# Turning x3 in blocks by way of DRAM, logits one step later, and four scalings on VectorE

## The chip, the cores and the metric

The kernel runs on one core of one Trainium2 chip. The metric is device time in microseconds (us) of the whole program, as the median of several executions. One more execution is taken by the hardware profiler; its views are what the text below quotes. The engines are TensorE (PE, and PEld for its weight loads), VectorE (DVE), ScalarE (ACT), GpSimd (POOL) and SyncE (SP). Each runs its own instructions in order. SP issues most of the DMAs, also in order, so that a DMA that has to wait holds up the ones behind it.

## The reference

A block of four layers on x of 8 x 512 tokens with 1024 features, all in float32. Each layer adds its output to x and begins with a layer norm.

```python
x = x + softmax_attention(layernorm(x), ...)           # 32 heads of 32
x = x + ffn(layernorm(x), weight, bias, centroids, assignments)
x = x + sigmoid_attention(layernorm(x), bv_q, bv_k, bv_v)   # 4 heads of 256, causal
x = x + ffn(layernorm(x), weight, bias, centroids, assignments)

def ffn(x, weight, bias, centroids, assignments):
    dots = softmax(x @ centroids.T / 0.1)              # 64 clusters
    hits = dots > 0.01
    dense = x @ weight.T + bias
    return where(any(hits, axis=1)[:, None] & any(hits, axis=0)[assignments][None, :], dense, 0)
```

In the sigmoid attention, Q, K and V are the normed x times one vector each; scores go through a sigmoid and a causal mask and are multiplied with V, head by head. The ffn needs the logits of every token against 64 centroids, the any() over all tokens of the block, and the dense product.

## The kernel before

The tokens are cut into 32 tiles of 128 (`NTILE`), four to a batch (`TPB`), eight batches. The stages follow each other: the softmax attention (up to about 2600 us), the first dense product with its gate (to about 3000), the sigmoid attention in 33 head steps (about 3001 to 3330), and the second dense product (to the end). x after the first ffn is called x2, after the sigmoid attention x3; both lie in DRAM as rows (`dr.x2`, `dr.x3`) and, after the norm, turned, with features in the partitions (`dr.xT2`, `dr.xT3`).

The change is in the head steps and in their first and last moments. Everything there is issued in the order in which the program is written (manual schedule); waits are put in by the framework, between engines, wherever a tile or a buffer of a pool is shared.

One head step s of the loop over `heads + 1` does this, in this order:

1. `load_head(s + 2)`: four DMAs on SP that bring the turned, normed x2 of a batch for one head (`cxT`, 128 KB each, three buffers).
2. `sig.scores(s)`: sixteen matmuls on TensorE (records "csc", L1300), the sigmoid on ScalarE (`at`, L1305), and four causal selects on POOL (L1308).
3. `by_token`: the second half of the cluster logits of finished tiles (TensorE L333, a copy on ScalarE L336). At the last tile of a batch it hands over the softmax steps (L357 to L380: VectorE, with one exponential on ScalarE, L361, which needs a table load, and the sigmoid after it another one).
4. `sig.keys(s + 1)`: ScalarE scales the turned x by q and k vectors (L1292).
5. `load_x2(s + 4)`: one DMA on SP into a ring of ten.
6. For the x3 tile normed in the step before, `turned`: for an even tile a fetch from DRAM, for an odd one eight transposes on TensorE (L277, "tp") with one copy on VectorE and one on ScalarE, and a store by POOL (L1447).
7. `x3_pieces(s - 5)`: statistics of the next x3 tile on VectorE, its root on POOL (L235), the store of x3 by POOL (L1473), the scaling on VectorE (L243).
8. `sig.values(s - 1)`: twenty records "o" on TensorE (L1319), whose results VectorE adds to x (L1325).
9. `by_cluster`: the first half of the logits (TensorE L325, a copy on ScalarE L329), for two tiles together after an odd tile.
10. `run_held`: softmax steps handed over in 3, and for an even tile the turn in blocks: VectorE turns 32 x 32 blocks of the tile (L294, `box`), and SP writes them to DRAM with four DMAs whose pieces are 128 bytes (L300), so that the tile lies turned in DRAM. The fetch of the next step reads it back.
11. `sig.value(s + 3)`: the scaling of one tile to V (ScalarE L240) and its product with the v vector (POOL L1286).

A tile t is normed in step t + 5 and turned or fetched in step t + 6. `in_blocks(t)` says which tiles go by way of DRAM: the even ones below 25. The logits' accumulators, the transposes and the turned maxima share three PSUM buffers (`ps_m`, tag "mm"). The pools for turned tiles (`Tpool`) and for normed ones (`npool`) have two buffers each.

Before the loop, the last pair of x2 tiles (30 and 31) goes through `x2_pair(15)`: gate, statistics, the factors `kept` (L1461). Its two scalings `n` run in step 1 and its turns in steps 2 and 3. The values of tiles 2 and 3 are made in step 0; those of 0 and 1 earlier, during the last dense product. All of these scalings go through `stage.rescale`, on ScalarE:

```python
def rescale(self, out, x, kept):
    self.nc.scalar.activation(out, x, AF.Identity, scale=kept[0], bias=kept[1])
```

Of the kernel before, what the change touches and what calls it, by code (L numbers as in the profile page):

```python
# [13 lines left out]
F32 = mybir.dt.float32  # L14
# [3 lines left out]
ALU = mybir.AluOpType  # L18
# [4 lines left out]
P = 128  # L23
B, S, H = 8, 512, 1024
NT = B * S
NC = H // P
TPB = S // P
NTILE = NT // P
# [5 lines left out]
HEADS_B, HD_B = 4, 256  # L34
# [34 lines left out]
class Filler:  # L69
# [38 lines left out]
    def run(self, count):  # L108

        while self.queue and count:  # L110
            count -= self._run_one() > 0
# [106 lines left out]
class Stage:  # L218
# [23 lines left out]
    def scale(self, out, x, mv, r, j):  # L242
        self.nc.vector.tensor_scalar(out, x, mv[:, j, 0:1], r[:, j : j + 1], ALU.subtract, ALU.mult)  # L243
# [1016 lines left out]
class SigmoidAttention:  # L1260
# [21 lines left out]
    def value(self, t, x, kept, ring=None):  # L1282
        pool, tag = (self.npools[t // TPB % 2], "n") if ring is None else (ring, "x2")
        v = self.v[t] = pool.tile([P, H], F32, tag=tag, name=f"cn_{t}")
        self.stage.rescale(v, x[t], kept)
        self.nc.gpsimd.tensor_tensor(v, v, self.v_bind, ALU.mult)  # L1286

    def keys(self, b, h):
# [44 lines left out]
def block_body(tc, long, dr, args, out):  # L1333
    x, xT_in, qkvw, qkvb, ow, ob, bv_q, bv_k, bv_v, wT, fbias, cT, assign = args
    nc = tc.nc
# [5 lines left out]
    def pools(stack, side):  # L1341
        def make(name, bufs, space=None):
            extra = dict(space=space) if space is not None else dict(side=side)
            return stack.enter_context(tc.tile_pool(name=name, bufs=bufs, reuse_waits="tile", **extra))

        return make
# [4 lines left out]
    stage, filler = Stage(tc, cst, small, ps_m), Filler()  # L1351
# [39 lines left out]
    kept = fixed.tile([P, 2, NTILE], F32, name="kept")  # L1391
    sel, pairs = {}, NTILE // 2

    def keep(t):
        return kept[:, 0, t : t + 1], kept[:, 1, t : t + 1]

    def dense_pools(stack):
        sb = pools(stack, right)
        return sb("f_load", 2), sb("f_sum", 1), sb("f_u", 4), pools(stack, left)("ps_d", 5, PSUM)
# [3 lines left out]
    dense1 = Dense(stage, weights, dense_pools(dense_stack), None, dr.xT1, dr.x1, hits1, sel)  # L1403
# [22 lines left out]
    a_outer.close()  # L1426

    sb = pools(middle, left)
    xring, npool, Tpool = sb("c_x", 10), sb("c_n3", 2), sb("c_T3", 2)
    dense1.xring = xring  # L1430

    def turned_tile(t, xT_dram):

        st = {}

        def xn():
            if "n" not in st:
                st["n"] = npool.tile([P, H], F32, tag="n3", name=f"n3_{t}")
            return st["n"]

        def xT():
            if "T" not in st:
                st["T"] = Tpool.tile([P, NC, P], F32, tag="T3", name=f"T3_{t}")
            return st["T"]

        def last():
            nc.gpsimd.dma_start(xT_dram[t], st["T"].rearrange("p c t -> p (c t)"))  # L1447

        return xn, xT, last

    def x2_pair(p):

        turns, tiles = [], (2 * p, 2 * p + 1)
        mv, cols = small.tile([P, TPB, 2], F32, tag="ln_mv", name="ln_mv")[:, :2], ts(p, 2)
        for t in tiles:
            dense1.gate(t)
            nc.gpsimd.dma_start(dr.x2[t], dense1.x[t])
        for k, t in enumerate(tiles):
            stage.stats(dense1.x[t], mv[:, k, :])
        stage.rstd(mv, 2, kept[:, 0, cols])  # L1460
        nc.vector.scalar_tensor_tensor(kept[:, 1, cols], mv[:, :, 0], -1.0, kept[:, 0, cols], ALU.mult, ALU.mult)  # L1461
        for t in tiles:
            xn, xT, _ = turned_tile(t, dr.xT2)
            scale = (0.0, lambda xn=xn, t=t: stage.rescale(xn(), dense1.x[t], keep(t)))
            turns.append((scale, stage.block_pieces(xn, xT, dr.xT2[t])))
        return turns

    def x3_pieces(t, blocks=False):


        xn, xT, last = turned_tile(t, dr.xT3)
        norm = stage.norm_pieces(lambda: x2[t], xn)
        norm.insert(1, (0.0, lambda: nc.gpsimd.dma_start(dr.x3[t], x2[t])))  # L1473
        later = held.extend if t < NTILE - TPB else None
        if blocks:
            made = []

            def box():
                if not made:
                    made.append(Tpool.tile([P, NC, P], F32, tag="T3", name=f"B3_{t}"))  # L1480
                return made[0]

            def fetch():
                nc.sync.dma_start(xT().rearrange("p c t -> p (c t)"), dr.xT3[t])

            held.extend(what for _, what in stage.block_pieces(xn, box, dr.xT3[t]))
            return norm, [(0.0, fetch)], hits2.pieces(t, xT, later)
        return norm, stage.turn_pieces(xn, xT, last, vector=(t < NTILE - TPB - 1)), hits2.pieces(t, xT, later)
# [4 lines left out]
    def run_held():  # L1493
        run(enumerate(held))
        held.clear()
# [4 lines left out]
    def load_x2(t):  # L1500
        if t < NTILE:
            x2[t] = xring.tile([P, H], F32, tag="x2", name=f"cx2_{t}")
            nc.sync.dma_start(x2[t], dr.x2[t])

    def load_head(s):
        if s < heads:
            sig.load_head(*divmod(s, HEADS_B), dr.xT2)
# [4 lines left out]
    for p in range(pairs):  # L1512
# [27 lines left out]
        if p > 0:  # L1540
            dense1.sums(p + 1)
        turns = x2_pair(p)
        dense1.load_turned(p + 2)
        dense1.load_x(p + 2)
# [2 lines left out]

    sig.open(pools(sig_stack, left))
    def in_blocks(t):
        return t % 2 == 0 and t < NTILE - TPB - 3  # L1550


    turned, normed, by_token, clustered = None, None, [], []
    for s in range(heads + 1):
        load_head(s + 2)
        if s < heads:
            sig.scores(*divmod(s, HEADS_B))
        run(by_token)
        by_token = []
        if s + 1 < heads:  # L1560
            sig.keys(*divmod(s + 1, HEADS_B))
        if s == 0:
            for t in range(2, TPB):
                sig.value(t, x2, keep(t))
        elif s == 1:
            run([scale for scale, _ in turns])
        load_x2(s + TPB)
        turned, normed = normed, None
        if turned is not None:
            run(turned[0])  # L1570
        if s > HEADS_B:
            t = s - HEADS_B - 1
            norm, *normed = x3_pieces(t, in_blocks(t))
            run(norm)
        if s > 0:
            sig.values(*divmod(s - 1, HEADS_B), x2)
        if turned is not None:
            clustered.append(turned[1])
            if not in_blocks(s - HEADS_B - 2):
                for by_cluster, _ in clustered:  # L1580
                    run([by_cluster])
                by_token = [second for _, second in clustered]
                clustered = []
        run_held()
        if s in (2, 3):
            run(turns[s - 2][1])
        t = s + TPB - 1
        if TPB <= t < NTILE:
            sig.value(t, x2, keep(t))
# [49 lines left out]
@with_exitstack  # L1639
def block_kernel(ctx, tc, x, xT_in, qkvw, qkvb, ow, ob, bv_q, bv_k, bv_v, wT, fbias, cT, assign, out):  # L1640
    long = ctx.enter_context(tc.tile_pool(name="long", bufs=1))
    dram = ctx.enter_context(tc.tile_pool(name="dram", bufs=1, space=DRAM))
    with tc.manual_schedule():
        block_body(tc, long, Scratch(dram), (x, xT_in, qkvw, qkvb, ow, ob, bv_q, bv_k, bv_v, wT, fbias, cT, assign), out)
# [33 lines left out]
```

## Time and profile before

| | |
|---|---|
| median of 3 runs | 3735.04 us (3732.08 to 3738.76) |
| the profiled execution's own time | 3736.19 us |
| its span | 3734.5 us |
| TensorE busy | 3683.2 us, 99% of the span |
| VectorE, ScalarE, POOL busy | 68%, 25%, 16% |
| mean DMA rate | 160 GB/s |

In the profile's lines, "L294 DVE STREAM_TRANSPOSE B<-n" is an instruction of line 294 on VectorE that writes tile B from n. "idle before <-X" tells how long the engine waited and for what. The chain of waits is followed back from the last instruction, at each step to what released it; time on the chain is time that the end depends on. In a table by windows the columns are the busy time of each engine, the granted clock of TensorE, the mean busy share of the 16 DMA engines, and GB/s.

### The profile page before, as it was taken

The numbers are of one execution on the slowest core, as the hardware profiler recorded it, in microseconds if no ns is written. First come the engines' busy times: TensorE is split into PE (matmuls) and PEld (weight loads), VectorE is DVE, ScalarE is ACT, GpSimd is POOL, SyncE is SP. The second block draws the span as 40 slices with busy tenths as digits, with TensorE's granted clock in tenths as the row PEclk, the third lists the DMA queues.
The fourth block names the chain that finished last, engine by engine and source line by source line (L and its number), as shares of the span: only waits on it lengthen the run. The fifth ranks groups of instructions, "written<-read, shape, count | busy, mean of one in ns | idle before, by whom it ended". The sixth has DMA issues, their size and how long they took to land.

```text
span 3734.5 us, 76359 instructions
## 1 busy us (share of the span) xinstructions
PE 3683.2 (99%) x32794; PEld 1877.6 (50%) x32794; DVE 2541.4 (68%) x3495; ACT 925.6 (25%) x1015; POOL 592.4 (16%) x572
## 2 busy tenths in 40 slices
PE   8999999999999999999999999998999999999999
PEld 4444454544545555445445445443444467774444
DVE  4777676777667667766767767665788845556656
ACT  1222222222222222222222222231111144430000
POOL 1222111111111111111111111111000045530000
PEclk9999999999999999999999999999999999999999
DMA  5345445645655455465465454456576667763332
GB/s 172 114 131 170 138 141 148 197 137 153 191 146 153 152 161 169 132 196 155 139 185 156 144 150 121 121 162 228 158 180 179 170 189 234 224 220 131 130 132 99
DMA packets 728641, 598.55 MB, mean 160 GB/s; under 512 B 322152, under 2 KB 574064, under 8 KB 728304
## 3 DMA queue, kind: packets, MB, share of 16 engines
q1 hardware_dynamic: 701072, 496.40, 46.5%
q0 software_dynamic: 22912, 81.54, 5.7%
q10 hardware_dynamic: 4320, 15.73, 1.0%
q8 instruction: 259, 4.24, 0.5%
q14 instruction: 78, 0.64, 0.1%
HBM read 459.30 MB, written 134.25 MB: 159 GB/s over the span
## 4 chain that ended last, share of the span: by engine, by line
PE 92%; DVE 4%; DMA 1%; issue 1%; SPq 1%; ACT 0%; POOL 0%; DVEq 0%; ACTq 0%; POOLq 0%
PE mm L554 41%; PE dense L1238 18%; PE sc L873 7%; PE av L929 6%; PE sc L905 6%; PE o L1319 4%; PE csc L1300 4%; PE sc L902 2%; PE logitsT L325 1%; PE den L941 1%; DVE nmax L874 1%; PE tp L277 1%; DVE sum L918 0%; PE tpm L554 0%; SPq L300 0%
## 5 line engine op out<-in xcount | busy, mean ns | idle before, releaser
L874 DVE TENSOR_REDUCE nmax<-sc 128x4 f32<-128x2048 f32 x256 | 586.0, 2289 | 291.1 <-PE sc L873 291.0
L907 ACT ACTIVATE pT<-sc 128x2048 f32<-128x2048 f32 x256 | 480.9, 1879 | 1131.2 <-PE sc L905 1126.5
L554 PE MATMUL mm<-xT,w 128*64 128x256 f32 (+1 forms) x3736 | 429.6, 384 | 1.1 <-DVE rden L944 1.1
L916 POOL TENSOR_TENSOR sum<-pT,pT 128x1024 f32<-128x1024 f32 x128 | 307.6, 2428 | 754.2 <-ACT pT L907 682.3
L554 PEld LDWEIGHTS mm<-xT,w 128*64 128x64 f32 (+1 forms) x3736 | 242.1, 135 | 206.2 <-issue 56.2
L554 PE MATMUL mm<-s,w 128*32 128x256 f32 (+1 forms) x3672 | 321.2, 381 | 1.4 <-DVE qk L144 1.4
L918 DVE TENSOR_TENSOR sum<-sum,pT 128x2048 f32<-128x2048 f32 x128 | 291.9, 2281 | 0.9 <-ACT pT L907 0.9
L873 PE MATMUL sc<-qk,qk 32*64 32x512 f32 x4096 | 285.1, 613 | 0.5 <-ACT pT L907 0.4
L142 DVE TENSOR_TENSOR u<-dense,u 128x512 f32<-128x512 f32 x223 | 147.9, 684 | 185.1 <-PE dense L1238 169.7
L554 PEld LDWEIGHTS mm<-s,w 128*32 128x32 f32 (+1 forms) x3672 | 180.5, 122 | 180.7 <-issue 69.1
L905 PE MATMUL sc<-qk,qk 32*128 32x512 f32 x2048 | 264.0, 589 | 0.0
L929 PE MATMUL av<-pT,v 128*32 128x512 f32 x2048 | 247.6, 601 | 0.0
L554 PE MATMUL mm<-ow,ctxT 128*32 128x512 f32 (+2 forms) x1276 | 246.5, 599 | 0.3 <-DMA ow<-o_T 0.3
L1238 PE MATMUL dense<-sum,s 128*128 128x512 f32 x512 | 231.8, 593 | 0.0
L554 PEld LDWEIGHTS mm<-w,xT 128*64 128x64 f32 (+1 forms) x3888 | 197.5, 133 | 62.2 <-issue 48.9
L554 PE MATMUL mm<-w,xT 128*64 128x128 f32 (+1 forms) x3888 | 218.1, 274 | 0.0
L144 DVE SCALAR_TENSOR_TENSOR qk<-mm,qkvb_s,qk 128x256 f32<-128x256 f32 x224 | 107.5, 480 | 125.4 <-PE mm L554 120.3
L554 PE MATMUL mm<-ow,c 128*64 128x512 f32 (+2 forms) x864 | 170.4, 596 | 2.7 <-DMA ow<-o_T 2.7
L1238 PE MATMUL dense<-wT_s,dT_b 128*128 128x512 f32 x384 | 171.2, 593 | 0.0
L1238 PE MATMUL dense<-wT_s,dT_a 128*128 128x512 f32 x384 | 171.1, 593 | 0.0
L554 PE MATMUL mm<-w,s 128*64 128x128 f32 x2688 | 162.5, 274 | 0.0
L554 PEld LDWEIGHTS mm<-w,s 128*64 128x64 f32 x2688 | 148.0, 137 | 22.9 <-issue 22.9
(232 smaller groups left out, 4468.2 us busy)
## 6 DMA issues: line engine op xcount, KB each, us to landing
w<-in_qkvw SPq DMA_DIRECT2D x252, 256.0 KB, 3.0
ow<-o_T SPq DMA_DIRECT2D x240, 256.0 KB, 3.6
w<-qk_T SPq DMA_DIRECT2D x224, 256.0 KB, 2.8
ow<-in_ow SPq DMA_DIRECT2D x180, 256.0 KB, 3.1
w<-v_T SPq DMA_DIRECT2D x112, 256.0 KB, 2.7
x<-in_x SPq DMA_DIRECT2D x32, 512.0 KB, 5.1
dT_a<-xT SPq DMA_DIRECT2D x32, 512.0 KB, 6.0
x_a<-x SPq DMA_DIRECT2D x32, 512.0 KB, 6.8
```

Of the source, the lines that this page charges most:

```text
L142: nc.vector.tensor_tensor(out, acc, other, ALU.add)
L554: nc.tensor.matmul(out[cols], lhsT[:, cols], rhs, **flags)
L873: nc.tensor.matmul(sc[ts(j, P // 2), h, :], st["q"][rows, cols], st["k"][rows, :], start=True, stop=True)
L874: nc.vector.tensor_reduce(st["nmax"][:, qt, :], sc, AX.X, ALU.max, negate=True)
L905: nc.tensor.matmul(sc[:, h, :], st["k"][rows, ts(kt, P)], st["q"][rows, :], start=False, stop=True)
L907: nc.scalar.activation(pT, sc, AF.Exp, scale=SCALE_A)
L916: nc.gpsimd.tensor_tensor(st["sum"][:, h, :], st["pT", 0][:, h, :], st["pT", 1][:, h, :], ALU.add)
L918: nc.vector.tensor_tensor(st["sum"], st["sum"], st["pT", kt], ALU.add)
L929: nc.tensor.matmul(st["av"][rows, :], st["v"][:, kt, rows], pT[:, h, :], start=(kt == 0), stop=(kt == TPB - 1))
L1238: nc.tensor.matmul(st["acc"], st["left"][LEFT[k]][:, c, :], self.w[RIGHT[k]][:, c, :], start=(c == 0), stop=(c == half - 1),)
L1300: nc.tensor.matmul(sc[:, AT_OFF[i] : AT_OFF[i] + n], k[:, c, ts(i, P)], xT[:, c, i * P :], start=(c == 0), stop=(c == 1),)
L1319: nc.tensor.matmul(acc[:, j - jj, :], at[:, start : start + P], self.v[b * TPB + i][:, cols], start=(i == 0), stop=(i == j),)
```

## The change

Four edits. All tiles below 25, odd ones too, are turned in blocks by way of DRAM. The box that holds the blocks comes from `npool`, and `Tpool` has three buffers instead of two. The logits of two tiles are still taken together, but after the next even tile has come, so one step later (from tile 25 on as before: at once). And four scalings go from ScalarE to VectorE: the values of tiles 2 and 3, and `n` of tiles 30 and 31.

```diff
     def value(self, t, x, kept, ring=None):
         v = self.v[t] = pool.tile([P, H], F32, tag=tag, name=f"cn_{t}")
-        self.stage.rescale(v, x[t], kept)
+        if 2 <= t < TPB:
+            self.nc.vector.tensor_scalar(v, x[t], *kept, ALU.mult, ALU.add)
+        else:
+            self.stage.rescale(v, x[t], kept)
         self.nc.gpsimd.tensor_tensor(v, v, self.v_bind, ALU.mult)
...
-    xring, npool, Tpool = sb("c_x", 10), sb("c_n3", 2), sb("c_T3", 2)
+    xring, npool, Tpool = sb("c_x", 10), sb("c_n3", 2), sb("c_T3", 3)
...
-            scale = (0.0, lambda xn=xn, t=t: stage.rescale(xn(), dense1.x[t], keep(t)))
+            def scale(xn=xn, t=t):
+                if p < pairs - 1:
+                    stage.rescale(xn(), dense1.x[t], keep(t))
+                else:
+                    nc.vector.tensor_scalar(xn(), dense1.x[t], *keep(t), ALU.mult, ALU.add)
+
+            scale = (0.0, scale)
...
-                    made.append(Tpool.tile([P, NC, P], F32, tag="T3", name=f"B3_{t}"))
+                    made.append(npool.tile([P, H], F32, tag="n3", name=f"B3_{t}").rearrange("p (c t) -> p c t", c=NC))
...
     def in_blocks(t):
-        return t % 2 == 0 and t < NTILE - TPB - 3
+        return t < NTILE - TPB - 3
...
         if turned is not None:
+            t, now = s - HEADS_B - 2, []
+            if t % 2 == 0:
+                now, clustered = clustered, []
             clustered.append(turned[1])
-            if not in_blocks(s - HEADS_B - 2):
-                for by_cluster, _ in clustered:
-                    run([by_cluster])
-                by_token = [second for _, second in clustered]
-                clustered = []
+            if not in_blocks(t):
+                now, clustered = now + clustered, []
+            for by_cluster, _ in now:
+                run([by_cluster])
+            by_token = [second for _, second in now]
```

## The prediction

> **What bounds the kernel now.** I read the page first (busy time, then the chain of waits), then the chain in order of time around the head steps, which the change rewrites, then the timeline at both ends of that stage, then the DMA share there.
>
> ```profile
> PE 3683.2 (99%) x32794; PEld 1877.6 (50%) x32794; DVE 2541.4 (68%) x3495; ACT 925.6 (25%) x1015; POOL 592.4 (16%) x572
> ...
> PE 92%; DVE 4%; DMA 1%; issue 1%; SPq 1%; ACT 0%; POOL 0%; DVEq 0%; ACTq 0%; POOLq 0%
> ```
>
> TensorE is the bound, and a gain must come from TensorE time. The chain in the head steps, one pair of steps:
>
> ```profile
> 3083.37 4.32 PE csc L1300 x16
> 3087.68 0.87 PE tp L277 x8
> 3088.56 4.32 PE o L1319 x20
> 3092.88 1.90 PE logitsT L325 x32
> 3094.77 4.51 PE csc L1300 x16
> 3099.29 0.39 PE logits L333 x4
> 3099.68 4.37 PE o L1319 x20
> ```
>
> The columns are start, length, work. From 3019 to 3322 the chain is TensorE alone, piece after piece; a pair lasts 3104.05 - 3083.37 = 20.68 us. Each odd tile's eight transposes ("tp") stand in it with 0.87 us. The stage's entry is different, as the timeline shows:
>
> ```profile
> 3007.96 2.36 ACT L240 ACTIVATE cn<-cx,kept 128x1024 f32<-128x1024 f32 x2
> ...
> 3013.09 1.03 POOL L1308 TENSOR_SCALAR_AFFINE_SELECT at<-at 128x128 f32<-128x128 f32 x4
> 3013.14 0.24 DVE L1461 SCALAR_TENSOR_TENSOR kept<-ln_mv,kept 128x2 f32<-128x2 f32 x1 [0.83 <-POOL kept L235]
> ...
> 3014.09 4.67 POOL L1286 TENSOR_TENSOR cn<-cn,v_bind 128x1024 f32<-128x1024 f32 x2
> 3014.49 2.36 ACT L240 ACTIVATE n<-x_a,kept 128x1024 f32<-128x1024 f32 x2
> ...
> 3016.50 1.99 PE L1319 MATMUL o<-cn,at 128*128 128x256 f32 x8 [0.65 <-POOL cn L1286]
> ...
> 3018.82 0.70 PE L1319 MATMUL o<-cn,at 128*128 128x256 f32 x2 [0.32 <-POOL cn L1286]
> ```
>
> Here POOL's products cn2 and cn3 hold TensorE: the first values() waits for each. ScalarE's scalings before them (3007.96) ended 3.8 us before POOL was free.
>
> **The change, term by term.**
>
> *Transposes removed: -10.45 us.* The odd tiles 1 to 23 lose eight transposes each: 12 x 0.87 = 10.45 us. Nothing in the chain is idle there, and between 3019 and 3067, where no "tp" stands yet, scores and values follow each other directly with the same 4.32 us; so all of it leaves the path. The PSUM copies (0.69 VectorE, 0.57 ScalarE) and POOL's store go too; they hid beside TensorE.
>
> *Block turns added, VectorE and the box.* A StreamTranspose is 1.23 us; VectorE is busy 125 of 233 us in these steps, so 1.23 - 0.69 more per pair is free. The box now shares a pool of two with n3, so a turn waits for the sends of the tile before. A turn ends about 2.7 us after values() (3072.19 to 3074.85); its sends take 3.0 us to issue and land in 3.2 at the median, some 9 us after values(); the next turn starts 10 us after it at the earliest. Free, with 1 us to spare.
>
> *SP's queue.* Each step now issues ten DMAs: four head loads (2.6 us), x2 (0.4), fetch (0.35), four sends (3.0), 6.4 us of a 9.9 us step. The head loads, now behind sends in every step, end their issue about 8.4 us after values() and land 4.5 us later; keys() needs them 13 us after values() at the earliest, and scores() 6 us later still. Free in the plain step.
>
> *DMA engines.* The shares are of 16 engines, first for the head steps 3088 to 3295, then for the dense stage 2750 to 2950:
>
> ```profile
> q1 hardware_dynamic: 67874, 31.10, 57.3%
> q0 software_dynamic: 4329, 15.76, 19.2%
> ...
> q1 hardware_dynamic: 87579, 25.89, 56.1%
> ```
>
> q0 carries only 512 KB tiles: 0.192 x 206.9 / 30 = 1.32 us of all engines each. Per pair q1 has 11.86 us: three 512 KB loads (3.97), eight head loads h and one tile's sends s: h + s = 7.89. In the dense stage 112.2 us hold 16 x loads (21.1), 16 dT loads with the same 512-byte pieces (half of h each) and 17 tiles' sends: 8h + 17s = 91.1. So s = 3.1 us, against 1.3 for the store that it replaces. The second fetch adds 1.3. A pair had 0.77 x 20.68 = 15.9 us of DMA work and gets 19.0 in 19.8 us: a share of 0.96. Can the engines run so full? Near the end of the stage they do, with TensorE never idle:
>
> ```profile
> 3309.00:3329.00 20.00, 20.00 (x131) 16.25 (x131) 14.20 (x34) 6.26 (x10) 6.22 (x12) 1.00 1.00 344
> ```
>
> The last three columns are granted clock, DMA share and GB/s: the engines are full for 20 us. I take 0 here, and put the other case under the rivals.
>
> *Logits one step later.* Tiles are still taken two at a time, but t-2 and t-1 at an even t. So the softmax of a batch moves from the step before a plain turn into a step with its own turn and sends, and stands ahead of that turn on VectorE. It ends 7.1 us after values() (3145.42 to 3152.54), so: turn 8.4, sends issued 11.4, heads issued 14.1, landed 18.1, keys (1.33) done 19.4; TensorE wants them at 19.8. Cover 0.4 us, five times. Between 0 and 5 x 1.1 (should landing take 1.5 us longer): I take +0.6.
>
> *The end, steps 31 and 32: +0.7 and +1.1.* Tile 25 is turned by TensorE in the step in which logits 22 and 23 come, which did not meet before. PSUM pool ps_m has three buffers, so the second half of the transposes waits for ScalarE's copy of logits 22, which stands behind the sigmoid (1.24): ready about 1.5 us after scores() instead of 0.8, +0.7. In step 32 the copy of logits 24 now stands behind the softmax's exponential of batch 5 with its table load (1.28 + 0.42, as at 3147.07): it frees the buffer for tile 26's second half 4.25 us after values(30) instead of 3.14, +1.1. Bounds: 0 if neither buffer is the one that is short, 2.8 if VectorE's late norm of tile 27 costs TensorE one more.
>
> *Four scalings on VectorE: +2.4.* On VectorE cn2 and cn3 come after L1461, at 3013.4; one takes 0.81 (the same form at L243). Without any contention cn2 is ready at 3014.2 + 0.1: POOL starts 0.2 later than now. But VectorE's four scalings, 3.2 us in a row, now run beside POOL's selects and products. No row has that pair; the nearest ones are
>
> ```profile
> L1457 POOL DMA_DIRECT2D x<-x_a x32: 534/546/595, 2651.9 to 3009.6; - x32
> L1473 POOL DMA_DIRECT2D x<-cx x32: 1000/1008/1030, 3052.7 to 3352.2; - x32
> L380 DVE TENSOR_TENSOR hits_b<-hits_b,some x7: 224/1294/1303, 3151.2 to 3369.0; 128x64 f32<-128x64 f32 x7
> ```
>
> POOL's DMA issue takes 1.01 instead of 0.55 where the 0.81 us scaling n runs beside it, and hits_b takes 1.3 instead of 0.22 while POOL multiplies (until 3152.46): they exclude each other. Taking turns after the selects: cn2 and cn3 on VectorE to 3015.7, product to 3018.05, n30 to 3018.8, product to 3021.15 instead of 3018.76: +2.4. Bounds: +0.2 without exclusion, +3.1 if the selects take turns as well. No gain faces it: ScalarE, which loses 4.7 us, made nobody wait here.
>
> The Trainium skill, "SBUF — State Buffer", section "Who interferes with whom", says that a two-port VectorE operation such as tensor_scalar and a GpSimd operation lock each other out for the whole instruction. No run here shows it for this pair; by the rule the term would be at least 1.6 and the sum -4.9 to -6.5, by the rows' lower bound the sum is -7.9.
>
> **Sum.** -10.45 + 0.6 + 0.7 + 1.1 + 2.4 = -5.65. The profiled span 3734.5 becomes 3728.85; its run took 3736.19, 1.15 above the median 3735.04, so I forecast 3735.04 - 5.65 = 3729.4.
>
> **Rivals.**
> - *The whole saving.* The end's waits and the exclusion are inferred, not seen: if one of them is nothing, the sum is between -10.45 and about -7.5: 3724.6 to 3727.5. For it: 300 us of chain without one gap. Against it: three buffers, and the rows on exclusion.
> - *DMA becomes the bound; slower.* Place: the sends, 128-byte pieces, in every step. If engines sustain a share f, a pair lasts 19.0 / f; with the other terms (4.8 / 12 = 0.4) the change loses from f below 19.0 / 20.28 = 0.94. At 0.90 a pair is 21.1: 12 x 0.43 = +5, with the other terms +10: 3745. For it: no pair of head steps seen here is above 0.79. Against it: nothing asked for more, and 1.00 over 20 us.
> - *The change doesn't do what it says:* excluded; the changed program issues twelve groups of transposes fewer, in these steps.
>
> **How the numbers follow.** About 0.2%, 7.5 us, is what a measurement here can tell from no change. Likeliest (0.55): 3726.8 to 3732, nearly all within 0.2%. Whole saving (0.27): faster. DMA (0.18): 3732 to 3750, 0.10 of it slower by over 0.2%. Faster: 0.27 + 0.07 = 0.34; slower 0.10; same 0.56. Range: 3723.5 (whole saving, less 1 for the spread of the runs) to 3740, beyond which about 0.1 lies.
>
> **What would show it.** Right: "tp" in the chain only from tile 25 on, a pair of 19.8 us, DMA share about 0.95; cn2's product ending near 3018, an idle TensorE of about 1 us before tp in steps 31 and 32. Wrong: "csc" waiting for keys and these for head loads in many steps (DMA), or values(0) ending at 3019.5 as now (no exclusion).

## The result, and the profile after

The changed kernel takes 3753.9 us (median of 5 runs, 3749.0 to 3757.32) against 3736.47 us in the same session: a ratio of 1.005, 95% interval 1.0037 to 1.0063. It is slower by some 17 us, where 5.6 us of gain were forecast. The profiled execution has a span of 3755.5 us, 21.0 more than before.

The page of the changed kernel, its busy times and the shares of its chain of waits:

```profile
PE 3683.4 (98%) x32698; PEld 1872.3 (50%) x32698; DVE 2554.1 (68%) x3499; ACT 914.6 (24%) x997; POOL 588.3 (16%) x560
...
PE 89%; DVE 4%; DMA 3%; SPq 1%; issue 1%; ACT 1%; POOL 0%; DVEq 0%; ACTq 0%; POOLq 0%
```

TensorE has 96 records fewer, the twelve groups of transposes, and yet the same busy time: what it does takes longer. DMA's share of the chain has gone from 1% to 3%. The chain in order of time shows where (start, length, work), first a pair of head steps that should last 19.8 us, then a long chain behind one wait:

```profile
3083.74 4.51 PE csc L1303 x16
3088.26 0.39 PE logits L333 x4
3088.65 4.37 PE o L1322 x20
3093.02 4.32 PE csc L1303 x16
3097.34 0.85 PE o L1322 x4
3098.19 5.25 DMA T<-xT
...
3103.49 1.09 PE logitsT L325 x16
...
3119.64 1.16 DVE B L294
...
3124.13 5.62 DMA xT<-B
...
3129.97 1.25 DVE B L294
...
3140.66 6.09 DMA T<-xT
3146.79 1.09 PE logitsT L325 x16
```

No "tp" stands here any more, as forecast. But logitsT now waits for the fetch of the second tile (T<-xT). Read the second chain from below: the fetch was issued at 3140.66, because SP was still issuing sends and head loads; those sends had waited for the turn (B) at 3129.97, and this for the sends of the tile before, which landed at 3129.8 after 5.62 us. SP's own timeline in the step before that fetch:

```profile
3131.24 5.38 SPq L300 DMA_DIRECT2D xT<-B  x4
3136.73 3.23 SPq L1280 DMA_DIRECT2D cxT<-xT  x4
3140.06 0.41 SPq L1512 DMA_DIRECT2D cx<-x  x1
3140.66 0.33 SPq L1493 DMA_DIRECT2D T<-xT  x1
3141.63 5.72 SPq L300 DMA_DIRECT2D xT<-B  x4
```

Four sends take 5.4 us to issue here and 5.1 at the median between 3088 and 3295 (3.0 before), and SP has hardly a gap in 10.4 us. The DMA engines, by windows (busy us of PE, PEld, DVE, ACT, POOL; then granted clock, DMA share, GB/s): first the head steps of the kernel before; then, of the changed kernel, the head steps, one stall, the 7 us behind it, another stall, and the 7 us behind that.

```profile
3067.00:3300.00 233.00, 233.00 (x1310) 180.37 (x1310) 125.19 (x271) 110.44 (x162) 117.80 (x172) 1.00 0.76 227
...
3067.00:3300.00 233.00, 218.41 (x1136) 164.19 (x1135) 120.92 (x253) 99.92 (x140) 102.25 (x147) 0.97 0.90 239
3144.29:3146.79 2.50, 0.00 (x1) 0.00 (x1) 1.80 (x5) 0.27 (x1) 0.59 (x1) 1.00 1.19 296
3146.79:3153.79 7.00, 7.00 (x42) 5.11 (x43) 2.61 (x4) 2.68 (x5) 2.34 (x1) 1.00 0.72 175
3231.80:3235.45 3.65, 0.00 (x1) 0.00 (x1) 2.47 (x7) 1.14 (x3) 1.53 (x2) 0.92 1.09 298
3235.45:3242.45 7.00, 7.00 (x24) 4.04 (x25) 2.56 (x4) 1.40 (x2) 2.34 (x1) 0.55 0.88 232
```

TensorE is busy 218.4 of 233 us (233.0 before) and the share is 0.90 (0.76 before). In the stalls the engines are full (1.19 and 1.09; over so short a stretch a share above 1 says no more than that). Behind the stall of 3.65 us the granted clock is 0.55: TensorE lost time twice.

The account, all in the two profiled executions. "Loop" is from the scores of step 2 to logitsT of tiles 24 and 25, "end" from there to the first dense product.

| part | before | after | difference |
|---|---|---|---|
| scores of step 2 begin | 3019.5 | 3021.4 | +1.9 |
| loop | 300.8 | 313.7 | +12.9 |
| end | 10.6 | 17.1 | +6.5 |

The sum, 21.3, is the difference of the spans but for 0.3. The experiment with wide pieces, below, shows that the loop without DMA stalls is 291.2, so the stalls cost 313.7 - 291.2 = 22.5 us: 14.6 us of idle TensorE between 3067 and 3300 (233 - 218.4), and about 8 us in which the same work took longer. Some 6.4 of these 8 lie behind three stalls at a lower clock (logitsT and scores at 3190, 3235 and 3282); most of the rest is logitsT in two halves, 1.09 us each instead of 1.90 for both.

### The profile page after: what moved, and what is told of

It reads as the page before. It is cut to its first block, busy times and chain, and to the rows that moved or that the text cites. A ratio compares the mean times of both kernels' runs of the same rounds, so it can differ in the third digit from the quotient of the medians.

```text
span 3755.5 us, 76186 instructions
## 1 busy us (share of the span) xinstructions
PE 3683.4 (98%) x32698; PEld 1872.3 (50%) x32698; DVE 2554.1 (68%) x3499; ACT 914.6 (24%) x997; POOL 588.3 (16%) x560
## 4 chain that ended last, share of the span: by engine, by line
PE 89%; DVE 4%; DMA 3%; SPq 1%; issue 1%; ACT 1%; POOL 0%; DVEq 0%; ACTq 0%; POOLq 0%
PE mm L554 41%; PE dense L1238 19%; PE sc L873 7%; PE av L929 6%; PE sc L905 6%; PE csc L1303 3%; PE o L1322 2%; PE sc L902 2%; PE den L941 1%; PE logitsT L325 1%; SPq L300 1%; DMA T<-xT 1%; DVE nmax L874 1%; DMA xT<-B 0%; DVE sum L918 0%
```

## Experiments on the sends, the buffer and the order

"Loop" is used as above, where the changed kernel has 313.7 us and the stall-free one 291.2; "middle" in the expectations is loop and end together less 0.7 us (330.1 in the changed kernel). Both are read from the one profiled execution. It lies within some 4 us of its kernel's median but for three: 5.8 above (pieces of 1 KB), 5.7 below (x3's stores) and 6.3 below (half of the odd tiles). Ratios are to the kernel before. The expectations set two theories against each other. By the work theory the DMA engines have more to move than a step lasts. By the other (buffer, queue or loop theory) the chain turn, sends, landing, fetch and its place in SP's order set the pace.

**A box of its own.** Does the box, which now shares a pool of two with n3, hold up the turn?

```diff
-                    made.append(npool.tile([P, H], F32, tag="n3", ...
+                    tag = ("rows", "rbias")[t % 2]
+                    made.append(fixed.tile([P, H], F32, tag=tag, ...
```

> The changed kernel, but the boxes alternate between the two tiles for rows and their bias, which lie idle in the head steps, so that a box no longer shares two buffers with n and a turn waits for sends two tiles back. Buffer theory (the loop turn, sends, landing, next turn sets the pace, 74.6 us of VectorE's waits in the changed kernel): the waits of logitsT for the fetch (31 us on 13 records) mostly go, the time falls by 20 us or more, to 3735 or less. Work theory (the 16 DMA engines have more to move than a step lasts, share 0.90 with full stretches): the turns come earlier, the sends land no earlier in the mean, the time stays within 8 us of 3754.

3760.17 us, ratio 1.0066 (1.0049 to 1.0082), loop 323.4. The turn's wait for sends is gone from the list of waits (67.3 us in 15 times in the changed kernel), and nothing is gained. The shared box is a link of the chain, not its cause.

**Wide pieces.** The sends write 32 whole rows of 4 KB each instead of 128-byte pieces; the tile then lies in another order in DRAM. Bytes and the number of DMAs are the same. What this kernel leaves out is the order of the elements, so its logits and its last dense product are others.

```diff
-            held.extend(what for _, what in stage.block_pieces(xn, box, dr.xT3[t]))
+            turn, _ = stage.block_pieces(xn, box, dr.xT3[t])
+
+            def send():
+                blocks = box().rearrange("p c t -> p (c t)")
+                for i in range(4):
+                    nc.sync.dma_start(dr.xT3[t][ts(i, 32)], blocks[ts(i, 32)])
+
+            held.extend([turn[1], send])
```

> The changed kernel, but the four sends of a box write rows of 4 KB instead of pieces of 128 bytes; the same bytes, as many DMAs, in the same places of the queue. Left out is the order of the elements: xT3 of the tiles below 25 is not the turned tile, so the logits and the last dense product are wrong. Work theory: a tile's sends cost 1.3 us of all engines instead of 3.1, the DMA share falls from 0.90 to about 0.8 with a pair at 19.8 us, SP issues the four in 2.5 us instead of 5.4, the waits of logitsT go, the time falls by about 25 us, to 3725 to 3732. Buffer theory: the landing of the sends gets shorter too, so it falls as well; what tells them apart is e1. If neither the work nor the landing matters (clock alone, or the order of the logits), it stays at 3754.

3734.64 us, ratio 0.9997 (0.9988 to 1.0007), loop 291.2. Its chain and its window of the head steps:

```profile
3083.20 1.90 PE logitsT L325 x32
...
3094.38 4.32 PE csc L1303 x16
3098.70 4.32 PE o L1322 x20
3103.01 1.90 PE logitsT L325 x32
```

```profile
3067.00:3300.00 233.00, 233.00 (x1254) 178.27 (x1253) 135.29 (x280) 108.02 (x153) 113.09 (x167) 1.00 0.80 262
```

A pair lasts 3103.01 - 3083.20 = 19.81 us, just what the removal of the transposes promised, at more GB/s (262) and a smaller share (0.80). So the 128-byte pieces of the sends cost all of the loop's stalls. SP issues a wide send in 0.42 us at the median, a narrow one in 0.67 with single ones up to 3.9 (between 3088 and 3295): with this alone, engine work and issue time can't be told apart. The experiment with x3's stores, below, says more on that.

**Later logits alone.** The kernel before, with only the order of the logits (and pools) of the change; odd tiles still by TensorE.

```diff
-            if not in_blocks(s - HEADS_B - 2):
+            t, now = s - HEADS_B - 2, []
+            if t % 2 == 0:
+                now, clustered = clustered, []
...
+            if t >= NTILE - TPB - 3:
```

> The kernel before with two edits of the change alone: logits one step later, and the box from the normed tiles' pool with three buffers for turned tiles. Odd tiles are turned by TensorE, the scalings stay on ScalarE. By the prediction's terms (0.6 for the softmax steps, 0.7 and 1.1 for steps 31 and 32) 2 us slower than before: 3738.5. By the profile of the changed kernel, where the logits of tile 24 wait for the last softmax step of batch 5 because their tile has one buffer, 4 to 6 us slower, about 3741, with TensorE idle 3 us ahead of the transposes of tile 26. If the collision of softmax and turn in one step is what stalls the changed kernel, 15 us or more slower.

3752.4 us, ratio 1.0047 (1.0032 to 1.0062), but by another mechanism: hardly a DMA stall and a full clock between 3067 and 3300. Two lines of its list of waits (waiter, releaser, us, times, longest):

```profile
PEld tp L277 <- ACT lg_b L336: 14.8, 13, 3.8
PE tp L277 <- ACT lg_b L336: 11.7, 13, 3.6
```

With the transposes kept, every odd step now has logits ahead of them, and the second half waits for a PSUM buffer: the stall of +0.7 that the forecast gave to step 31, here in every odd step. So the edits of the change belong together, and this run says nothing on the softmax in front of the turn.

**Scalings back on ScalarE, and scalings alone.** The first is the changed kernel without the four scalings on VectorE, the second the kernel before with only them.

```diff
-        if 2 <= t < TPB:
-            self.nc.vector.tensor_scalar(v, x[t], *kept, ALU.mult, ALU.add)
-        else:
-            self.stage.rescale(v, x[t], kept)
+        self.stage.rescale(v, x[t], kept)
...
```

> The changed kernel with the four scalings back on ScalarE. Exclusion of VectorE and POOL (prediction: 2.4 us lost): POOL's two products take 4.67 us instead of 5.55 and scores of step 2 start about 2 us earlier, at 3019.4 instead of 3021.4; the time falls by 2 us, which the rounds will hardly tell. No exclusion: both stay.

> The kernel before with the four scalings on VectorE and nothing else. Forecast's theory (VectorE and POOL take turns, so that V of tiles 2 and 3 comes later): the scores of step 2 begin 2 to 3 us later than at 3019.4, the time is 2 to 3 us above before. Rival (the scalings cost nothing; the 1.6 us that the start of step 2 was later in the changed kernel has another cause): scores of step 2 at 3019 to 3019.6, time within 1 us of before.

Back on ScalarE: 3758.17 us (1.0049 to 1.0079), no better than the changed kernel. Alone: 3738.33 us, ratio 1.0008 (0.9999 to 1.0017), +2.7 us by the medians, an interval that still holds no change; its loop is 300.8 as before. The profiles say more than the times. The timeline of the changed kernel at the entry:

```profile
3013.17 1.96 POOL L1311 TENSOR_SCALAR_AFFINE_SELECT at<-at 128x128 f32<-128x128 f32 x4
...
3013.39 1.59 DVE L1286 TENSOR_SCALAR cn<-cx,kept 128x1024 f32<-128x1024 f32 x2
...
3014.90 3.55 DVE L1471 TENSOR_SCALAR n<-x_a,kept 128x1024 f32<-128x1024 f32 x2
3015.10 5.55 POOL L1289 TENSOR_TENSOR cn<-cn,v_bind 128x1024 f32<-128x1024 f32 x2
```

Beside VectorE's scalings POOL's four selects take 1.96 us instead of 1.03 and its two products 5.55 instead of 4.67; VectorE's two n take 3.55 instead of 2 x 0.81. The two engines hold each other up, which was the forecast's assumption. With the scalings back on ScalarE the two products take 4.66 us again, but the scores of step 2 begin at 3021.1, hardly earlier, and not at 3019.4 as expected: that run came to the entry later. Measured inside the entry, from POOL's first select to the scores of step 2, the price is plain: 6.2 to 6.3 us in all ten kernels of this study with the scalings on ScalarE, 8.1 to 8.6 in all ten with them on VectorE, so 1.8 to 2.3 us.

**Pieces of 1 KB for the heads.** A head's tile lies tile by tile, so that a load writes 1 KB in one piece instead of 512 bytes.

```diff
-        xT = self.xT[b, h] = self.xTp.tile([P, 2, S], ...
+        xT = self.xT[b, h] = self.xTp.tile([P, TPB, 2, P], ...
...
-            self.nc.sync.dma_start(xT[:, :, ts(i, P)], src)
+            self.nc.sync.dma_start(xT[:, i], src)
...
```

> The changed kernel, with the tile of a head laid out tile by tile, so that each head load writes pieces of 1 KB instead of 512 bytes; nothing else. Work theory (the DMA engines are the limit in the head steps, and the pieces' number sets their work): the heads' share of the engines falls by 1 to 1.5 us per pair, so part of the stalls goes: the scores of step 2 to the transposes of tile 27 take 312 to 325 us instead of 330.1, the time falls from 3754 to 3738 to 3749. Rival (the sends alone hold up the fetch: their own 128-byte pieces are slow, whatever else the engines do): middle 328 to 332 us, time 3750 to 3757.

3756.09 us, ratio 1.0057 (1.0043 to 1.007), loop 320.9 (from an execution 5.8 us above the median): a miss for the work theory, which expected fewer stalls. The DMA packets between 3088.5 and 3295.4 fall from 106773 to 93807 and the share per MB by only 1.4% (0.899 for 49.1 MB, 0.874 for 48.4). From 512 bytes to 1 KB nothing is won; the 128-byte pieces are another matter. The Trainium skill, "DMA: Bandwidth & Descriptors", section "Specifications", puts the least transfer for full rate at 512 bytes and says that below it a read-modify-write is done. This run and the one with wide pieces agree with the 512 bytes; no run here shows the read-modify-write.

## Experiments on the end and on the queues

**A second buffer for the logits, and both together.** One more 1 KB buffer, so that two batches' logits don't share one.

```diff
+                pool = self.pool if b % 2 else getattr(self, "lgp", self.pool)
...
+    hits2.lgp = sb("c_lg", 1)
```

> The changed kernel, with a second buffer for the logits of a batch (batches 0, 2, 4 and 6 in one, 1, 3, 5 and 7 in the other). Theory (in step 32 the copy of logits 24 waits for the last step of the softmax, since the batch before holds the only tile): between the logitsT of step 32 and values(31) the idle time of TensorE falls from about 4.3 us to about 1, the clock there stays at full speed, the time falls by 3 to 5 us to 3748 to 3751. Rival (the copy waits for the exponential and its table load alone): idle time stays at 4 us, time within 2 us of 3754.

> The changed kernel with both: 1 KB pieces of the heads, and a second buffer for the logits. Work theory: the two gains add up, 3733 to 3745, near the kernel before, below it only if all stalls in the head steps go. Rival (neither matters): 3750 to 3757.

With the buffer alone 3750.82 us (1.0028 to 1.0056); with both 3755.56 (1.0039 to 1.007), so the heads' pieces add nothing here either. The end is 11.8 us in each, instead of 17.1. The chain in step 32, first of the changed kernel, then with the buffer:

```profile
3337.48 1.28 ACT L361
...
3338.78 0.42 ACT lg_b L361
...
3341.10 0.50 DVE some L379
...
3341.68 0.23 ACT lg_b L336
...
3341.96 1.11 PE tp L277 x4
```

```profile
3336.75 0.53 ACT L362
...
3338.04 0.42 ACT lg_b L362
3338.46 0.12 ACT lg_b L337
...
3338.62 0.66 PE tp L277 x4
```

Without it, the copy of logits 24 (L336) waits until VectorE's last step of the softmax (L379) has read the only logits tile. With it, it waits for the exponential alone, and the end is 1.2 us above before's 10.6: the forecast's +1.1.

**Heads on ScalarE's queue.** The four loads of a head are issued by ScalarE; the second kernel is the control, the same move in the kernel before.

```diff
-            self.nc.sync.dma_start(xT[:, :, ts(i, P)], src)
+            self.nc.scalar.dma_start(xT[:, :, ts(i, P)], src)
```

> The changed kernel, with the four loads of a head issued by ScalarE instead of SP; bytes and pieces stay. Queue theory (SP issues ten DMAs one after the other and is occupied for the whole step, 5.5 us of it by the four sends, so the fetch is issued late; the engines could do more): SP has 3.8 us to spare per step, the stalls go, csc(2) to the transposes of tile 27 takes 306 to 315 us instead of 330, the time is 3731 to 3742. Work theory (the 128-byte pieces fill the DMA engines, and SP's sends are slow because of that): the heads' packets are as many, the middle stays at 322 to 334 us, the time at 3745 to 3760.

> The kernel before, with the four loads of a head issued by ScalarE; the price of that move by itself. Both theories: no stall in before, so 3734 to 3738; above 3740 if ScalarE's issues (about 3 us per step) come ahead of a sigmoid or a copy that TensorE waits for.

3753.99 us (1.0034 to 1.0064), loop 314.3, as in the changed kernel; the control 3736.37 (0.9992 to 1.0011). SP now has time to wait, in 207 us of head steps above all for the sends to land:

```profile
SPq L1493 <- DMA xT<-B: 53.1, 23, 5.7
SPq L300 <- DVE B L294: 19.2, 12, 4.0
SPq L300 <- DMA cxT<-xT: 17.0, 8, 5.5
```

A full queue on SP was therefore not what held the fetch up. With the heads in a queue of their own their share is seen too: in the control 18.0% of 206.9 us for 80 loads, 3.7 us per pair, against 4.8 by the forecast's two equations.

**x3's stores elsewhere.** POOL's 512 KB stores of tiles below 25 move to the dense stage; SP's list is untouched. What this kernel leaves out is the right contents: the rows stored there are x2.

```diff
+            if t < NTILE - TPB - 3:
+                nc.gpsimd.dma_start(dr.x3[t], dense1.x[t])
...
-        norm.insert(1, (0.0, lambda: nc.gpsimd.dma_start(dr.x3[t], x2[t])))
+        if t >= NTILE - TPB - 3:
+            norm.insert(1, (0.0, lambda: nc.gpsimd.dma_start(dr.x3[t], x2[t])))
```

> The changed kernel, with POOL's store of x3 left out of the head steps for the tiles below 25; a store of the same size stands in the dense stage before (so x3 of these tiles is x2 in DRAM, and the output is not the reference's). SP's list of DMAs is untouched. Work theory (the engines' total work, 0.9 and more of their time, is the limit): 2.6 us less per pair, the middle takes 308 to 318 us, the time falls by 12 to 20 us to 3734 to 3742. Queue theory (SP's order and the sends' own slowness): the middle stays at 325 to 332 us, time 3748 to 3756.

3743.03 us, ratio 1.0016 (1.0007 to 1.0025), a microsecond above the expected range; loop 297.5: stalls of 6.3 instead of 22.5 us. This profile is of an execution 5.7 us below the median; by the medians the kernel is 10.9 us faster than the changed one. Its head steps:

```profile
3067.00:3300.00 233.00, 228.74 (x1227) 173.32 (x1227) 133.53 (x273) 106.64 (x151) 88.00 (x137) 1.00 0.83 202
```

Sends, fetches and SP's order are the same, and four sends take as long to issue as in the changed kernel (5.2 us at the median, against 5.1). So slow issue alone doesn't make the stalls; at least about half of them come from what the sends have to share the engines with. With the stores POOL's own 1.0 us of issuing each of them has left the head steps too; whether that has a part in it was not tried.

**Candidates with the loop's links cut.** The first has the heads on ScalarE, the second logits buffer and the scalings back on ScalarE. The other four let POOL issue the fetch at the end of the step, so that SP's next sends don't stand behind it: that edit alone; with a box of its own, the buffer and ScalarE's scalings; with the first candidate; and with all of it.

```diff
-                nc.sync.dma_start(xT().rearrange("p c t -> p (c t)"), dr.xT3[t])
+                nc.gpsimd.dma_start(xT().rearrange("p c t -> p (c t)"), dr.xT3[t])
...
+        run(fetch)
```

> The changed kernel with the heads issued by ScalarE, the second buffer for the logits, and the four scalings back on ScalarE. Queue theory: 3725 to 3733, faster than both kernels. Work theory: 3741 to 3755.

> The changed kernel, with the fetch of a turned tile issued by POOL at the end of the step instead of by SP near its start; nothing else. Loop theory (on SP the fetch waits until the sends of its tile have landed, and the sends of the next tile stand behind it: issue 5.4 and landing 5.6 us make a period above the 9.9 us of a step): SP never waits for a landing, the sends of the next tile leave earlier, the middle (scores of step 2 to transposes of tile 27) falls from 330 to 312 to 324 us, the time to 3738 to 3749. Work theory (the engines can't do more than about 0.9 of their time with such pieces): middle 326 to 334 us, time 3748 to 3758.

> The changed kernel with POOL's late fetch, a box of its own for the blocks (two buffers), the second buffer for the logits, and the four scalings on ScalarE; the heads stay on SP. Loop theory: as with POOL's fetch alone and without its waits for the box, middle 306 to 315 us, time 3728 to 3738. Work theory: middle 315 to 325, as in the candidate with the heads on ScalarE (317.7), time 3740 to 3748.

> The candidate before (heads by ScalarE, second logits buffer, scalings on ScalarE; 3742.1 us, middle 317.7) with POOL's late fetch. Loop theory: SP has only sends and x2 left, stalls remain only where the turn waits for the box: middle 306 to 312 us, time 3727 to 3735. Work theory: middle 315 to 320, time 3739 to 3745.

> The same with a box of its own too: no wait is left between one tile's sends and the next turn. Loop theory: no stall in the loop, pairs of 19.8 us, middle 302 to 308 us, time 3725 to 3732, faster than both kernels. Work theory: the DMA engines' share stays near 0.92, the middle at 315 to 320, time 3739 to 3745.

| kernel | us | interval of the ratio | loop | PE busy of 233 | share |
|---|---|---|---|---|---|
| heads, buffer, scalings | 3742.1 | 1.001 to 1.0029 | 306.6 | 222.5 | 0.92 |
| POOL's fetch alone | 3760.78 | 1.0055 to 1.0085 | 320.6 | 213.7 | 0.89 |
| with box, buffer, scalings | 3754.57 | 1.0035 to 1.0068 | 318.1 | 217.0 | 0.90 |
| with the first candidate | 3748.75 | 1.0023 to 1.0053 | 307.8 | 219.8 | 0.93 |
| with all | 3742.57 | 1.0014 to 1.0033 | 304.3 | 221.8 | 0.94 |

The loop theory falls: with fetch, box and heads all off the chain of SP, TensorE is still idle for 11.2 of 233 us. The first and the last meet the times of the work theory; the other three lie above both theories' ranges. Two neighbouring windows of the last kernel:

```profile
3210.00:3230.00 20.00, 18.37 (x103) 14.02 (x102) 10.06 (x22) 8.06 (x12) 9.21 (x17) 1.00 1.09 285
3230.00:3250.00 20.00, 18.61 (x106) 14.55 (x105) 11.04 (x24) 9.80 (x15) 10.82 (x16) 1.00 0.80 206
```

The engines are full in one stretch and not in the next, and the mean over the head steps never came above 0.94. Only three of the five have a shorter loop than the changed kernel. Most of what the first and the last win there (7.1 and 9.4 us) is clock: no stall between 3060 and 3345 is above 2.01 us, the clock stays at 1.00, and idle TensorE in 3067 to 3300 falls only from 14.6 to 10.5 and 11.2 us. The rest of their gain in time is the end, by the second logits buffer.

**Half of the odd tiles.** Tiles 3, 7, 11 and so on by way of DRAM, 1, 5, 9 by TensorE, and transposes ahead of the logits. Both kernels have the second logits buffer and ScalarE's scalings; the second has the heads on ScalarE too.

```diff
...
-        return t < NTILE - TPB - 3
+        return t % 4 != 1 and t < NTILE - TPB - 3
...
+        if normed is not None and not in_blocks(s - HEADS_B - 2):
+            run(normed[0])
+            normed[0] = []
         run(by_token)
```

> Only half of the odd tiles go by way of DRAM (3, 7, 11, 15, 19, 23; the tiles 1, 5, 9 and so on are turned by TensorE), a tile's transposes stand before the logits of a step instead of behind them, the logits have the second buffer, and the four scalings are on ScalarE. Work theory (stalls come where the engines are asked for more than about 0.93 of their time): 34.9 us of DMA work in two pairs of 40.5 is 0.86, so few stalls or none; 6 x 0.87 = 5.2 us of transposes are gone: middle 305 to 309 us, time 3729 to 3735. Rival (any odd tile that goes by way of DRAM costs more than its transposes, since the sends of two neighbouring steps collide): middle 312 to 320, time 3737 to 3745.

> The same with the heads issued by ScalarE. Work theory: as without that move, 3729 to 3735, middle 305 to 308. Rival: 3734 to 3742, middle 310 to 316.

3765.38 us (1.0065 to 1.009) and 3751.17 (1.0026 to 1.0054): slower than both theories allow, at a mean share of 0.79 and 0.81. In part that is a stall of their own: the logits now wait for the copy of the transposes behind the sigmoid, 0.84 us in each such step. But of the 18.3 us of idle TensorE in the first, 11.9 are four waits for a fetch. Two of these stalls:

```profile
3186.36:3189.37 3.01, 0.00 (x0) 0.00 (x1) 1.89 (x5) 0.58 (x2) 0.68 (x1) 0.94 1.14 304
3279.93:3283.95 4.02, 0.00 (x1) 0.00 (x0) 3.07 (x8) 1.48 (x3) 1.53 (x2) 1.00 1.13 334
```

The engines are full in all four (1.12 to 1.20), whatever the mean. So a mean share over many steps doesn't foretell the stalls.

No kernel here is clearly faster than the one before.

## Why the prediction was wrong

*Transposes, -10.45:* right. The loop with wide pieces is 300.8 - 291.2 = 9.6 shorter, which is -10.45 with the +0.7 of step 31 (shown there as well); hardly anything is left for the +0.6 of the softmax where the sends are quick.

*DMA engines, "I take 0 here":* the step that failed, +22.5 us in the loop. The sum of work was nearly right: 0.90 of a pair of 21.7 us (19.81 and a twelfth of 22.5) is 19.5 us, against 19.0 forecast. (How it splits was not: the heads are 3.7, not 4.8, so a tile's sends, what is left of 7.89, are 4.2, not 3.1; with 4.2 the forecast itself would have been 20.1 us in a pair of 19.8.) What was wrong is that a share of 0.96 can be had for nothing. The 20 us at 1.00 that I showed for it were mostly loads of the dense stage, for which nobody waited yet. And "no pair of head steps seen here is above 0.79" misread the profile. Cut into pairs from 3083.37, the kernel before goes up and down, 0.80 to 0.84 and 0.70 to 0.75, as in these two:

```profile
3166.09:3186.77 20.68, 20.68 (x118) 15.97 (x117) 9.30 (x20) 7.29 (x12) 9.63 (x15) 1.00 0.84 248
3186.77:3207.45 20.68, 20.68 (x118) 15.97 (x117) 13.51 (x29) 12.53 (x17) 11.23 (x16) 1.00 0.73 212
```

A mean of 0.96 left no room for that. Full engines with no one waiting show what engines can move, not what a transfer on the path of a consumer waits. The highest mean over the head steps seen with TensorE waiting is 0.94.

*Box, "1 us to spare", and SP's queue, "6.4 us of a 9.9 us step":* both used issue and landing times of the quiet kernel. With the engines busy four sends issue in 5.1 instead of 3.0 us at the median and land in 5.0 instead of 3.2, and SP is occupied for the whole step. Neither is the cause alone, as the experiments with a box of its own and with the heads on ScalarE show.

*The rival "DMA becomes the bound":* this came nearest, though the wait it named, scores for keys and these for head loads, is not the one: the only waits that TensorE's matmuls show in the head steps are those of logitsT for the fetch (14.5 us, 6 times). At 0.90 its formula gave a pair of 21.1 us, measured 21.7, but no one share f holds for all kernels here: one ran at 0.94, and another stalled at 0.79. It was priced at 3745 because the end's waits and the clock were too small in it, and given 0.18 because the full window spoke against it.

*Step 32, +1.1:* right for the wait that was named, wrong in all. Only one buffer exists for a batch's logits, and I had looked only at PSUM's three. End: +6.5, of it about 3.6 idle and 2.3 in values(31) at a low clock (6.6 instead of 4.3 us).

*Four scalings, +2.4:* right, if a little large. The exclusion is seen in the durations, and from POOL's first select to the scores of step 2 it costs 1.8 us in the changed kernel, and 1.8 to 2.3 in all ten with these scalings. The start of step 2 by itself would not show it: it lies between 3015.6 and 3023.4 in the profiles of all kernels here.

*The clock:* not in the forecast at all, about 6.4 us in the loop and 2 at the end.

What stays open: how the engines' work and the chain turn, sends, fetch share the blame. That other traffic matters and that no single queue or buffer does is shown. With half of the odd tiles the engines are full in each stall for a fetch at a mean of 0.79; what bunches the transfers there is not settled. What the softmax ahead of the turn adds was not tried by itself.

## What to carry to other kernels

When a change trades an engine's work for DMA work that someone waits for, take the landing and issue times from a stretch in which the DMA engines are as full as they will be, and don't read a forecast mean of 0.96 as room: look at how far the share swings around its mean, for every kernel here at a mean of 0.88 to 0.94 stalled, and two at 0.79 and 0.81 did so too. Before a step is moved across another, list every buffer it touches with its number of copies, SBUF tiles too, and not only the pool that first comes to mind. And count a stall of the busiest engine with what it does to its clock.

## What was not expected of the hardware

TensorE's clock after a stall. In all kernels of this study, of 82 stalls of 0.8 to 1.65 us between 3060 and 3345 none was followed by a lower clock in the next 7 us; of 38 between 1.65 and 3.3 us, 23 were; of 17 longer ones, all were. Where it fell, the mean clock of those 7 us was 0.54 to 0.79. One stall of 3.65 us stretched the next scores from 4.5 to 6.7 us:

```profile
3235.45 1.98 PE L325 MATMUL logitsT<-T,cT_s 128*64 128x128 f32 x16 [3.65 <-DMA T<-xT]
3237.36 6.72 PE L1303 MATMUL csc<-cxT,k 128*128 128x512 f32 x16
```

The Trainium skill, "TensorE: Matmul & The Clock Gate", section "The HAM clock gate", has the clock fall to half after an idle window of about 3.4 us, and has these windows run freely. The 17 long stalls agree in kind; that 23 stalls of less than 3.3 us also cost clock, the shortest of 1.82 us, is more than it says. The clock's records in the traces say how: from 100 us on, the granted clock of a run falls only on a grid of 3.413 us and stays low for one or two of its windows. Counted on that grid between 3020 and 3345, the next window ran at half clock after all 39 full-clock windows in which TensorE was idle for 1.9 us or more, after 5 of 21 with 1.5 to 1.9 us, and after none of 206 with 0.1 to 1.5 us. So a window need not be idle as a whole: a stall costs clock here when it empties rather more than half of one, and one that falls across two windows, as the stall of 2.50 us shown above, may cost none.

And the issue of a DMA is no constant: a send of 128 KB in 128-byte pieces took SP between 0.58 and 3.9 us in the changed kernel between 3088 and 3295 (0.67 at the median), and four in a row 5.1 us at the median, where the kernel before took 3.0.
